# A six-layer decoder on one core: expert sums as seven block products, and two groups in turns

## The chip, the cores and the metric

The kernel runs on one core of a Trainium2 chip. Times are device microseconds (us) of one execution. Engines are named as the profile does: PE is TensorE (PEld its weight loads), DVE VectorE, ACT ScalarE, POOL GpSimd, SP the queue that issues most DMAs.

## What is computed

Sixteen sequences of 128 tokens with 256 features pass six sub-layers, each of the form `x = layernorm(x + f(x))`, all in float32:

- layer 0: attention with 16 heads of 64, causal mask, biases
- layer 1: 8 experts of hidden width 512; every token goes through every expert
- layer 2: two shared experts of hidden width 128 and 16 routed ones of 64 (top 2 by a softmax router)
- layer 3: attention with 16 heads of 16 and a band mask
- layer 4: cross attention with 16 heads of 16 to a context of 128 positions
- layer 5: 8 experts of hidden width 512 with GELU; again every token goes through every expert

The two layers that the change is about, cut to what matters:

```
# layer 1 (gate[b,s,e] sums the context's weights of the entries that chose e)
h   = relu(einsum('bsd,eid->bsei'))            # proj_in
out = einsum('eid,bsed->bsei', proj_out, h) summed over e with gate

# layer 5
h   = gelu(einsum('nd,edh->neh', xf, w1) + b1)
y   = einsum('neh,ehd->ned', h, w2) + b2
out = (y * norm_g[:, None, None]).sum(axis=1)
```

So each of these layers ends in a sum over 8 experts of a product of (tokens x 512) by (512 x 256).

## The kernel before

The sixteen sequences are four groups of four (`GB = 4`), a group has `T = 512` tokens. For a group, x is kept with tokens on partitions and, transposed, as xT with features on partitions. A layer of a group is a Python generator (`attention0`, `ensemble0`, `experts0`, `attention1`, `cross1`, `experts1`) that emits instructions and yields the TensorE time that the emitted piece should take. A `Weaver` mixes two such streams, main and side, in the proportion of the numbers given to it, and short streams (`tail`: the transposes of the next xT and the routing) go first when they are ready. `UNTIL` lets a stream wait until a given planned time. Layer n of a group starts when the tail of layer n - 1 has written xT (`written[g]`).

Main streams are the attentions: (0,0) alone first, then (0,1), (0,2), (0,3), then (3,g), (4,g) for each group. The side stream is called dense: (1,0), (2,0), (1,1), (2,1), (1,2), (2,2), (1,3), (2,3), then (5,0) to (5,3); what is left of it at the end runs alone. The pair is (layer, group). From the emitted program the framework then makes the queue of each engine, and two instructions of an engine needn't keep the order of the text, unless `keep_in_program_order` or `together` asks for it.

Layers 1 and 5 use `accumulate`. A piece i of 32 is one expert's quarter of hidden features. `hidden(i)` makes 128 hidden features of the 512 tokens (two matmuls of 512 columns at L289) and evicts them to SBUF (VectorE at L650 in layer 1, ScalarE at L813 in layer 5). Then four matmuls of 256 columns (L589) add this quarter's product to the four token blocks in two PSUM banks (tag M), over all 32 pieces. The result has tokens on partitions, and `Norm.add` reads it from PSUM at L265 or L267. Each matmul of the code is two records in the profile.

PSUM has 8 banks: H (2), M (2), O (2) and S (one buffer of two). Weights of an expert, up and down, lie in one slot of 8 KB a partition, of which there are three (`wp`, bufs=3); SP loads them in the order of the program as slots come free. Attention weights have three slots of their own.

`softmax` emits for a unit of scores: a minimum with the mask on VectorE (L311), a maximum (L317 or L319), one exponential a head on ScalarE (L325), a reciprocal on VectorE (L330), the product on GpSimd (L331). `weights_T` transposes e on TensorE (L51) and ScalarE copies it (L340). In layers 3 and 4 GpSimd also makes kb (L456), one head's keys spread over a block, ahead of the scores (L464).

Of the kernel before, what the change touches and what calls it, by code (L numbers as in the profile page):

```python
# [27 lines left out]
def kernel(ctx: ExitStack, tc: tile.TileContext, a: dict, out: bass.AP):  # L28
# [3 lines left out]
    wp = ctx.enter_context(tc.tile_pool(name="dense", bufs=3))  # L32
# [37 lines left out]
    def load_w(pool, name, *parts):  # L70
        w = pool.tile([P, 2048], F32, tag=pool.name, name=name)
        views, at = [], 0
        for part in parts:
            p_, r, c = part.shape
            v = w[:, at:at + r * c].rearrange("p (r c) -> p r c", r=r)
            nc.sync.dma_start(out=v, in_=part)
            views.append(v)
            at += r * c
        return views

    def load_quad(j):
# [3 lines left out]
            ap, f"wquad{j}", a["L0_attn_W_Q"][:, :, cols], a["L0_attn_W_K"][:, :, cols],  # L85
            a["L0_attn_W_V"][:, :, cols], a["L0_attn_W_O"][:, 2 * j:2 * j + 2, :],
        )

    def load_expert0(e):
        return load_w(wp, f"we0_{e}", a["L0_xattn_proj_in"][e], a["L0_xattn_proj_out"][e])  # L90

    def load_expert1(e):
        return load_w(wp, f"we1_{e}", a["L1_ffn_w1"][e], a["L1_ffn_w2"][e])

    def load_experts(t):

        if t == 0:
            return load_w(wp, "ws", a["L0_ffn_wg_s"], a["L0_ffn_wu_s"], a["L0_ffn_wd_s"])
        cols = slice((t - 1) * D, t * D)
        return load_w(  # L100
            wp, f"wr{t}", a["L0_ffn_wg_r"][:, :, cols], a["L0_ffn_wu_r"][:, :, cols],
            a["L0_ffn_wd_r"][:, 2 * t - 2:2 * t, :],
        )
# [61 lines left out]
    bv0 = spread("L0_attn_b_V")  # L165
    bo0 = spread("L0_attn_b_O")
    ctxs = cp.tile([P, NB, P], F32, tag="ctx", name="ctx")
    nc.gpsimd.dma_start(out=ctxs, in_=a["ctx_512"].rearrange("b k s -> k b s"))
# [4 lines left out]
    bv1 = spread("L1_xattn_bv")  # L173
# [17 lines left out]
    class Weaver:  # L191
# [23 lines left out]
        def weave(self, main, side=None, us=(1.0, 1.0)):  # L215
# [4 lines left out]
            while not main.over:  # L220
# [15 lines left out]
    def transposed(x, xT=None):  # L236
# [3 lines left out]
        for c in range(KC):  # L240
# [5 lines left out]
            else:  # L246
                nc.scalar.copy(xT[:, c, :], pt)
        return xT
# [42 lines left out]
    def values(xT, w, k, evict):  # L291

        v = p3.tile([P, GB, D], F32, tag="v", name="v")
        for b in range(0, GB, 2):
# [7 lines left out]
            evict(v[:, b:b + 2, :], pv)  # L302
# [3 lines left out]
    def softmax(s, seen):  # L306

        n = 2 * s.shape[2]
        if seen is not None:
            sm = p2.tile([P, n, P], F32, tag="s", name="sm")  # L310
            nc.vector.tensor_tensor(  # L311
                sm.rearrange("p (s h) k -> p s h k", s=2), s,
                seen.unsqueeze(1).unsqueeze(1).to_broadcast([P, 2, n // 2, P]), ALU.min,
            )
        nmax = sp.tile([P, n], F32, tag="nmax", name="nmax")
        if seen is not None:
            nc.vector.tensor_reduce(nmax, sm, AX.X, ALU.max, negate=True)  # L317
        else:
            nc.vector.tensor_reduce(  # L319
                nmax.rearrange("p (s h) -> p s h", s=2), s, AX.X, ALU.max, negate=True  # L320
            )
        e = p3.tile([P, n, P], F32, tag="p", name="e")
        total = sp.tile([P, n], F32, tag="total", name="total")
        for h in range(n):
            nc.scalar.activation(  # L325
                e[:, h, :], sm[:, h, :] if seen is not None else s[:, h // (n // 2), h % (n // 2), :],
# [16 lines left out]
    def attention0(x, xT, g):  # L343
# [4 lines left out]
        def project_quad(j):  # L348
# [16 lines left out]
            def with_bias(v, pv):  # L365
                nc.vector.tensor_tensor(
                    v, pv, bv0[:, j * D:(j + 1) * D].unsqueeze(1).to_broadcast([P, 2, D]),
                    ALU.add,
                )

            v = yield from values(xT, wv, KC, with_bias)
# [27 lines left out]
        for n in range(len(units) + 5):  # L399
# [17 lines left out]
            if m in eT:  # L417
# [14 lines left out]
                nc.scalar.copy(zT[m], pz)  # L432
# [14 lines left out]
    def attention16(x, qT, kT, v, wo, bo, seen):  # L447
# [22 lines left out]
        def weigh(b, c, eT):  # L470
# [15 lines left out]
            nc.scalar.activation(half_z, pz[:, 0, :], AF.Copy, scale=even[:, 0:1])  # L486
# [13 lines left out]
        for n in range(len(units) + 4):  # L500
            if n < 8:
                e[n] = yield from scores(*units[n])
                at["e", n] = weaver.now + 14.0
                yield 1.06
            m = n - 1
# [6 lines left out]
            m = n - 3  # L512
# [4 lines left out]
            m = n - 2  # L517
# [21 lines left out]
    def attention1(x, xT):  # L539
        wqkv, wo = load_w(ap, "wa1", a["L1_attn_Wqkv"], a["L1_attn_Wproj"])  # L540
# [7 lines left out]
        v = yield from values(xT, wqkv[:, :, 2 * D:3 * D], KC, nc.scalar.copy)  # L548
        yield from attention16(x, qT, kT, v, wo, bp1, band)

    def cross1(x, xT, g):
        wq, wk, wv, wo = load_w(
            ap, "wx1", a["L1_xattn_Wq"], a["L1_xattn_Wk"], a["L1_xattn_Wv"], a["L1_xattn_Wo"]
        )
        pc = bank("H")
        for b in range(GB):
            transpose(pc[:, b * P:(b + 1) * P], ctxs[:, g * GB + b, :])
        cT = p2.tile([P, 1, T], F32, tag="s", name="cT")
# [10 lines left out]
        def with_bias(v, pv):  # L569
            nc.vector.tensor_tensor(  # L570
                v, pv, bv1.unsqueeze(1).to_broadcast([P, 2, D]), ALU.add
            )

        v = yield from values(cT, wv, 1, with_bias)
        yield from attention16(x, qT, kT, v, wo, bo1, None)
# [22 lines left out]

    gates_of = {}

    def gates0(g):
# [5 lines left out]
        cx = ctxs[:, g * GB:(g + 1) * GB, :].rearrange("p b s -> p (b s)")  # L607
        held = dp.tile([8, T], F32, tag="gates", name="gatesd", bufs=NG)
        for q in range(2):
# [16 lines left out]
            sums = p3.tile([P, T], F32, tag="hT", name="sums")  # L626
# [8 lines left out]
    def ensemble0(x, xT, g):  # L635
        gates = {}
        w_exp0 = {}

        def hidden(i):
            e, c = divmod(i, 4)  # L640
            if c == 0:
                w_exp0[e] = load_expert0(e)
# [320 lines left out]
```

## Time and profile before

| what | us |
|---|---|
| median of 3 runs | 1867.82 |
| lowest, highest | 1865.88, 1871.24 |
| the profiled execution, its own time | 1863.81 |
| span of its records, first to last | 1862.1 |
| PE busy in it | 1805.6 |
| ACT busy | 750.1 |
| DVE busy | 648.7 |
| POOL busy | 363.0 |

The profile is one execution, recorded by the hardware profiler. A row of a group reads: line, engine, operation, tile written from tiles read, shape and count, then busy us and mean ns of one, then the idle time of the engine ahead of it and what ended that. A row of a table of stretches has busy us of PE, PEld, DVE, ACT and POOL with the number of instructions, the granted TensorE clock, the busy share of the DMA engines and GB/s. A row of waits names who waited for whom, with the total, the number of times and the longest.

### The profile page before, as it was taken

The page shows a single profiled execution, that of the slowest core. Times are in us where ns is not written, and L with a number is a line of the kernel's source. Part 1 is how long each engine was busy: PE and PEld are TensorE (multiplying, and loading weights), DVE is VectorE, ACT ScalarE, POOL GpSimd, SP SyncE. Part 2 cuts the span into 40 slices and gives each one's busy share as a digit, 9 for nine tenths or more (in the row PEclk, how much of TensorE's full clock was granted, in tenths as well). Part 3 has the DMA queues.
Part 4 walks back from the last instruction along what each step waited for, and adds up shares of the span by engine and source line. Part 5 has one row for each costly group of instructions (what it writes and reads, how often), then busy time and mean ns, then how long its engine had stood idle before and what let it go on. Part 6 is the DMA issues. An engine that isn't in the chain of part 4 may idle for free.

```text
span 1862.1 us, 21229 instructions
## 1 busy us (share of the span) xinstructions
PE 1805.6 (97%) x7794; PEld 1111.5 (60%) x7794; DVE 648.7 (35%) x1359; ACT 750.1 (40%) x2229; POOL 363.0 (19%) x297
## 2 busy tenths in 40 slices
PE   6999999999999999999899999899999999999998
PEld 3656666566666656656455665465565655556665
DVE  3453334434333525343425444333223222312101
ACT  2541222342312333241452423527748468475221
POOL 4210001121101112122332213223122122221000
PEclk9999999999999999999899999999999999999999
DMA  6021123122221132122123121121111111111220
GB/s 233 24 86 57 57 74 102 58 85 74 99 89 37 44 120 101 63 71 66 41 79 108 63 91 34 58 93 66 46 63 57 46 68 46 57 46 68 80 76 26
DMA packets 67272, 132.72 MB, mean 71 GB/s; under 512 B 6600, under 2 KB 34304, under 8 KB 67168
## 3 DMA queue, kind: packets, MB, share of 16 engines
q1 hardware_dynamic: 66240, 129.20, 20.5%
q0 software_dynamic: 928, 2.17, 0.4%
q8 instruction: 62, 1.02, 0.2%
q14 instruction: 42, 0.34, 0.1%
HBM read 129.04 MB, written 2.29 MB: 71 GB/s over the span
## 4 chain that ended last, share of the span: by engine, by line
PE 81%; issue 7%; ACT 5%; DVE 5%; DMA 1%; POOL 1%; SPq 0%; POOLq 0%; DVEq 0%; ACTq 0%
PE psH L289 34%; PE psM L589 23%; PE psH L298 4%; PE psO L51 4%; PE psS L464 3%; PE psH L393 3%; ACT e L325 2%; PE psS L384 2%; PE psO L426 2%; PE psO L476 2%; PE psH L495 1%; PE psH L51 1%; DMA wquad<-in_L_attn_W_Q 1%; ACT L325 1%; DVE x L281 1%
## 5 line engine op out<-in xcount | busy, mean ns | idle before, releaser
L589 PE MATMUL psM<-we,hT 128*128 128x256 f32 x2048 | 496.2, 383 | 3.1 <-ACT hT L813 3.1
L289 PE MATMUL psH<-xT,we 128*128 128x512 f32 x1024 | 488.3, 598 | 1.3 <-DVE hT L650 1.3
L589 PEld LDWEIGHTS psM<-we,hT 128*128 128x128 f32 x2048 | 380.7, 190 | 153.1 <-issue 95.1
L331 POOL TENSOR_TENSOR e<-e,inv 128x512 f32<-128x512 f32 (+1 forms) x128 | 188.2, 1471 | 792.6 <-DVE inv L330 728.2
L289 PEld LDWEIGHTS psH<-xT,we 128*128 128x128 f32 x1024 | 187.4, 190 | 159.9 <-issue 142.0
L325 ACT ACTIVATE e<-sm,nmax 128x128 f32<-128x128 f32 x512 | 198.5, 389 | 152.9 <-DVE nmax L317 152.5
L340 ACT COPY eT<-psO 128x512 f32<-128x512 f32 x192 | 106.0, 586 | 207.2 <-PE psO L51 206.7
L650 DVE SCALAR_TENSOR_TENSOR hT<-psH,gt 128x512 f32<-128x512 f32 x128 | 88.1, 689 | 214.1 <-PE psH L289 214.1
L813 ACT ACTIVATE hT<-psH,b 128x512 f32<-128x512 f32 x128 | 86.9, 687 | 177.1 <-PE psH L289 176.5
L289 PE MATMUL psH<-xT,wquad 128*128 128x512 f32 x256 | 117.7, 603 | 1.3 <-DVE qT L357 0.8
L51 PEld LDWEIGHTS psO<-ident,e 128*128 128x128 f32 x768 | 88.4, 143 | 49.4 <-issue 32.1
L51 PE MATMUL psO<-ident,e 128*128 128x128 f32 x768 | 111.0, 281 | 5.0 <-POOL e L331 4.9
L289 PE MATMUL psH<-xT,wr 128*128 128x512 f32 x256 | 115.8, 594 | 0.0
L456 POOL TENSOR_TENSOR kb<-kT,hm 128x512 f32<-128x512 f32 x64 | 66.9, 1046 | 189.4 <-PE psS L464 128.7
L330 DVE RECIPROCAL inv<-total 128x4 f32<-128x4 f32 (+1 forms) x128 | 23.9, 187 | 216.6 <-ACT e L325 214.0
L325 ACT ACTIVATE e<-psS,nmax 128x128 f32<-128x128 f32 x256 | 90.1, 379 | 21.3 <-DVE nmax L319 20.9
L325 ACT ACTIVATION_READ_ACCUMULATOR e<-sm,nmax 128x1 f32 x512 | 95.8, 187 | 0.0
L464 PE MATMUL psS<-kb,qT 64*128 64x512 f32 x256 | 84.5, 646 | 7.0 <-ACT e L325 6.7
L279 POOL TENSOR_TENSOR rstd<-ve,mhalf 128x4 f32<-128x4 f32 x24 | 24.3, 1012 | 310.0 <-DVE ve L277 309.4
L317 DVE TENSOR_REDUCE nmax<-sm 128x4 f32<-128x512 f32 (+1 forms) x96 | 82.8, 863 | 2.7
L289 PEld LDWEIGHTS psH<-xT,wquad 128*128 128x128 f32 x256 | 47.2, 191 | 58.3 <-issue 50.2
L289 PEld LDWEIGHTS psH<-xT,wr 128*128 128x128 f32 x256 | 48.0, 190 | 49.5 <-issue 46.3
(155 smaller groups left out, 1802.9 us busy)
## 6 DMA issues: line engine op xcount, KB each, us to landing
we<-in_L_ffn_w SPq DMA_DIRECT2D x64, 512.0 KB
we<-in_L_xattn_proj_in SPq DMA_DIRECT2D x32, 512.0 KB
we<-in_L_xattn_proj_out SPq DMA_DIRECT2D x32, 512.0 KB
gt<-gatesd SPq DMA_DIRECT2D x32, 256.0 KB
cw<-combd SPq DMA_DIRECT2D x64, 128.0 KB
wquad<-in_L_attn_W_Q SPq DMA_DIRECT2D x16, 256.0 KB
wquad<-in_L_attn_W_K SPq DMA_DIRECT2D x16, 256.0 KB
wquad<-in_L_attn_W_V SPq DMA_DIRECT2D x16, 256.0 KB
```

What stands on the lines that cost most here:

```text
L51: return nc.tensor.transpose(out_, in_, ident[:n, :n])
L289: mm(pt, lhsT=w[:, c, cols], rhs=xT[:, c, :], start=c == 0, stop=c == KC - 1)
L298: mm(pv[:, i, :], lhsT=xT[:, c, (b + i) * P:(b + i + 1) * P], rhs=w[:, c, :], start=c == 0, stop=c == k - 1,)
L317: nc.vector.tensor_reduce(nmax, sm, AX.X, ALU.max, negate=True)
L325: nc.scalar.activation(e[:, h, :], sm[:, h, :] if seen is not None else s[:, h // (n // 2), h % (n // 2), :], AF.Exp, bias=nmax[:, h:h + 1 ...
L331: nc.gpsimd.tensor_tensor(e, e, inv.unsqueeze(2).to_broadcast([P, n, P]), ALU.mult)
L340: return eT, nc.scalar.copy(eT, pt)
L456: nc.gpsimd.tensor_tensor(kb, kT[:, c, at].unsqueeze(1).to_broadcast([P, 4, P]), hm4.unsqueeze(2).to_broadcast([P, 4, P]), ALU.mult,)
L464: mm(s[:, k, :], lhsT=qT[rows, c, at], rhs=kb[rows].rearrange("p h k -> p (h k)"), start=True, stop=True,)
L589: step = mm(acc[b], lhsT=held[:, b * P:(b + 1) * P], rhs=down(i), start=i == 0 and b % 2 == 0, stop=i == n - 1, skip_group_check=True,)
L650: nc.vector.scalar_tensor_tensor(out=hT, in0=ph, scalar=0.0, in1=gates[e], op0=ALU.max, op1=ALU.mult)
L813: nc.scalar.activation(hT, ph, AF.Gelu, bias=b1[:, i:i + 1])
```

## The change

The sum of an expert's product is made by Strassen's scheme. Hidden features and output features are halved, and tokens too: a (tokens x hidden) by (hidden x features) product becomes two by two blocks, and seven products of blocks replace eight. One operand of a product is a sum or difference of two blocks of the hidden values, the other one of the down weights.

- The weight blocks (7 of 256 columns) are computed on GpSimd when the first group reaches an expert, stored to HBM from GpSimd's queue, and loaded from there by the other three groups (`load_blocks`).
- The hidden sums are made for an expert by VectorE, two of the five by GpSimd (`sums`).
- `multiply` issues the products in four phases, each of two products into one bank M (one in the last phase); VectorE then adds the bank to an accumulator in SBUF. The phases of expert e - 1 alternate with the four hidden pieces of expert e.
- At the end `products_end` combines the seven sums to four blocks, transposes them to tokens on partitions and adds them to x. It runs as a short stream, followed by the layer's tail.
- Up weights have three slots of 4 KB, blocks two slots of 7 KB. To make room, the context is loaded by group, the masked scores are written into e itself, and the biases of v go onto zT, which in layer 0 VectorE writes now instead of ScalarE.
- In layers 3 and 4 the transposes follow the scores two units later, not one.
- Dense order: two groups take layer 1 in turn, then both layer 2. The first main stream is (0,0), (0,1) with nothing beside it, and three mixed stretches of two groups follow.

The diff, cut to its core:

```diff
-    wp = ctx.enter_context(tc.tile_pool(name="dense", bufs=3))
+    wp = ctx.enter_context(tc.tile_pool(name="dense", bufs=2))
...
+    def load_up(name, *parts):
+        return load_w("up", 1024, name, *parts, bufs=3)
+
+    def load_down(name, *parts):
+        return load_w("down", 14 * P, name, *parts)
...
-    bv0 = spread("L0_attn_b_V")
+    bv0 = const("bv0", [P, 8], a["L0_attn_b_V"].rearrange("o (c p) -> p (o c)", p=P))
-    ctxs = cp.tile([P, NB, P], F32, tag="ctx", name="ctx")
-    nc.gpsimd.dma_start(out=ctxs, in_=a["ctx_512"].rearrange("b k s -> k b s"))
...
-            evict(v[:, b:b + 2, :], pv)
+            nc.vector.tensor_copy(v[:, b:b + 2, :], pv)
...
-                nc.scalar.copy(zT[m], pz)
+                nc.vector.tensor_tensor(
+                    zT[m], pz, bv0[:, 2 * j:2 * j + 2].unsqueeze(2).to_broadcast([P, 2, P]), ALU.add
+                )
...
-            m = n - 1
+            m = n - 2
             if m in e:
                 yield UNTIL, at["e", m]
...
+    def load_blocks(layer, e, g, w):
+        if (layer, e) in in_hbm:
+            got, = load_down("wb", in_hbm[layer, e])
+            return got.rearrange("p s (q d) -> p s q d", q=2)
+        raw, = load_up("raw", w)
+        raw = raw.rearrange("p (q l) (j d) -> p q l j d", l=2, j=2)
+        t = wp.tile([P, 7, 2 * P], F32, tag="down", name="wb0")
+        blocks = t.rearrange("p s (q d) -> p s q d", q=2)
+        for s, (_, (one, two, op)) in enumerate(PRODUCTS):
+            if two is None:
+                step = nc.gpsimd.tensor_copy(blocks[:, s], raw[:, :, one[0], one[1], :])
+            else:
+                step = nc.gpsimd.tensor_tensor(
+                    blocks[:, s], raw[:, :, one[0], one[1], :], raw[:, :, two[0], two[1], :], op
+                )
+            if s == 0:
+                together(step, *transposed_by[g])
+        held = dp.tile([P, 7, 2 * P], F32, tag=f"wb{layer}", name="wbd", bufs=8)
+        nc.gpsimd.dma_start(out=held, in_=t)
...
+        def sums(e, phase):
+            t = None
+            for s in range(2 * phase, min(2 * phase + 2, 7)):
+                one, two, op = PRODUCTS[s][0]
+                if two is None:
+                    parts[e, s] = half(e, one)
+                    continue
+                if t is None:
+                    t = p3.tile([P, 2, 2, 2 * P], F32, tag="cm", name="cm")
+                parts[e, s] = t[:, s % 2]
+                engine = nc.gpsimd if s in (3, 5) else nc.vector
+                engine.tensor_tensor(t[:, s % 2], half(e, one), half(e, two), op)
+
+        def multiply(e, phase):
+            pm = bank("M").rearrange("p (s t) -> p s t", s=2)
+            slots = range(2 * phase, min(2 * phase + 2, 7))
+            for q in range(2):
+                for s in slots:
+                    step = mm(
+                        pm[:, s % 2, :], lhsT=blocks[e][:, s, q, :], rhs=parts[e, s][:, q, :],
+                        start=q == 0 and s % 2 == 0, stop=q == 1, skip_group_check=True,
+                    )
...
+            to = acc[:, slots[0]:slots[-1] + 1, :]
+            if e == 0:
+                nc.vector.tensor_copy(to, pm[:, :len(slots), :])
+            else:
+                nc.vector.tensor_tensor(to, pm[:, :len(slots), :], to, ALU.add)
+
+        for e in range(9):
+            if e < 8:
+                blocks[e] = blocks_of(e)
+                h[e] = p2.tile([P, 4, T], F32, tag="h", name="h")
+            if e > 0:
+                sums(e - 1, 0)
+                sums(e - 1, 1)
+            for c in range(4):
+                if e < 8:
+                    hidden(h[e][:, c, :], up[e], e, c)
+                    yield 1.72
+                    if c == 1 and e < 7:
+                        up[e + 1] = load_up_of(e + 1)
+                if e > 0:
+                    if c < 2:
+                        sums(e - 1, c + 2)
+                    multiply(e - 1, c)
+                    yield 1.72 if c < 3 else 0.86
+        finish(acc)
+
+    def products_end(acc, norm, scale):
+        t = p3.tile([P, 2, 2, 2 * P], F32, tag="cm", name="y")
...
+        nc.gpsimd.tensor_tensor(c12, m3, m5, ALU.add)
+        nc.vector.tensor_tensor(c11, m4, m5, ALU.subtract)
+        nc.vector.tensor_tensor(c11, c11, m1, ALU.add)
+        nc.vector.tensor_tensor(c11, c11, m7, ALU.add)
+        nc.gpsimd.tensor_tensor(c21, m2, m4, ALU.add)
+        nc.vector.tensor_tensor(c22, m1, m2, ALU.subtract)
+        nc.vector.tensor_tensor(c22, c22, m3, ALU.add)
+        nc.vector.tensor_tensor(c22, c22, m6, ALU.add)
...
-        (1, 0), (2, 0), (1, 1), (2, 1), (1, 2), (2, 2), (1, 3), (2, 3),
+        (1, 0), (1, 1), (2, 0), (2, 1), (1, 2), (1, 3), (2, 2), (2, 3),
         (5, 0), (5, 1), (5, 2), (5, 3),
     ))
-    weaver.weave(Stream(chain((0, 0))))
+    weaver.weave(Stream(chain((0, 0), (0, 1))))
     weaver.short.append(Stream(sum_biases()))
...
+    weaver.weave(Stream(chain((0, 2), (0, 3))), dense, (81.0, 150.0))
+    weaver.weave(Stream(chain((3, 0), (4, 0), (3, 1), (4, 1))), dense, (68.0, 150.0))
+    weaver.weave(Stream(chain((3, 2), (4, 2), (3, 3), (4, 3))), dense, (68.0, 150.0))
+    weaver.weave(dense, last=True)
```

## The prediction

> **What bounds the kernel now.** I read the page's head and its chain first, then the time order of TensorE in the stretch with the least company, then tables by stretch, last the waits of the engines that get new work.
>
> ```profile
> span 1862.1 us, 21229 instructions
> ...
> PE 1805.6 (97%) x7794; PEld 1111.5 (60%) x7794; DVE 648.7 (35%) x1359; ACT 750.1 (40%) x2229; POOL 363.0 (19%) x297
> ...
> PE 81%; issue 7%; ACT 5%; DVE 5%; DMA 1%; POOL 1%; SPq 0%; POOLq 0%; DVEq 0%; ACTq 0%
> ```
>
> TensorE is busy for 97% and makes up 81% of the chain; no other engine passes 40%. Busy is not yet peak, so the price of a matmul comes from starts, in the stretch in which layer 5 runs alone:
>
> ```profile
> 1759.68 1.89 PE L589 MATMUL psM<-we,hT 128*128 128x256 f32 x8
> 1761.41 1.88 PE L289 MATMUL psH<-xT,we 128*128 128x512 f32 x4
> 1763.13 1.89 PE L589 MATMUL psM<-we,hT 128*128 128x256 f32 x8
> ```
>
> Each matmul of the code is two records. Eight records, four matmuls of 256 columns, take 1.73 us from start to start: 0.431 us each; two of 512 columns take 1.72 us. Here TensorE does not wait at all. Where it does wait shows in a table of stretches (busy columns PE, PEld, DVE, ACT, POOL, then the granted clock):
>
> ```profile
> 895.00:920.00 25.00, 17.29 (x92) 9.40 (x91) 14.28 (x41) 15.12 (x61) 9.71 (x7) 0.80 0.11 29
> 1150.00:1180.00 30.00, 23.03 (x111) 12.77 (x109) 20.12 (x57) 15.71 (x62) 11.79 (x8) 0.89 0.09 28
> 1750.00:1850.00 100.00, 100.00 (x350) 66.26 (x349) 0.00 (x0) 20.08 (x30) 0.00 (x0) 1.00 0.15 54
> ```
>
> The first two are changes of layer: an expert sum of a group has ended, its routing isn't there yet, and only attention is left to run. TensorE idles 7.7 and 7.0 us, at a lower clock. VectorE does nothing in the third.
>
> **The change part by part.**
>
> *Seven products for eight.* An expert pass of layer 1 or 5 (8 experts, 4 groups, 2 layers: 64 passes) issues 14 down matmuls of 256 columns for 16. Shape and operands' sizes stay, so the price stays: 64 x 2 x 0.431 = -55.2 us, on the path since TensorE bounds. A pass falls from 8 x 1.72 = 13.8 to 12.9 us.
>
> *Transposes at the end.* The sums now come out with features on partitions: 8 transposes for each of 8 group-layers. Four transposes of e start 0.43 us ahead of what follows (168.37 to 168.80 in the time order), so 64 x 0.11 = +7.0 us.
>
> *Evictions and sums.* Before, PSUM held the sum over all experts. Now each pass evicts four phases into SBUF (three of 512 columns, one of 256) and makes five sums of hidden halves, three on VectorE, two on GpSimd. The nearest rows:
>
> ```profile
> L311 DVE TENSOR_TENSOR sm<-psS,causal 128x512 f32<-128x512 f32 x64 | 44.1, 689 | 51.4 <-PE psS L384 51.4
> L265 DVE TENSOR_TENSOR x<-psH,x 128x256 f32<-128x256 f32 x96 | 40.3, 420 | 83.4 <-PE psH L495 48.6 <-PE psH L393 34.2
> L756 POOL TENSOR_TENSOR hT<-sg,cw x32: 1262/1270/1383, 361.1 to 1247.8; 128x512 f32<-128x512 f32 x32
> ```
>
> VectorE: 3 x 0.69 + 0.42 + 3 x 0.69 = 4.6 us a pass, 292 us in all; with 64 zT evictions taken from ACT (64 x 0.42 = 27), v (6) and the final combination (8 x 6 x 0.42 = 20) it goes from 649 to about 994 us, 55% of the span. GpSimd: 128 sums x 1.27 = 163 us; and for the first group of a layer 7 block operations of 256 elements (about 0.65 us each, half of the 512 row) and a store issue (the 1 MB ctx load cost 1.19 us) for 16 experts, 89 us: 363 to some 625 us, 34%. What hides this is the time of a pass: each sum is made one phase ahead and has about 5.2 us of TensorE work (three pieces of 1.72) before it is read, each bank two phases. If that cover is gone, 1 us of lateness a pass costs 64 us.
>
> *Whether they come late* is the unknown term. Two waits block the queues concerned:
>
> ```profile
> POOL e L331 <- DVE inv L330: 728.2, 117, 29.5
> DVE inv L330 <- ACT e L325: 214.0, 82, 8.1
> ```
>
> GpSimd stands at the softmax product, 6.2 us on average, VectorE at the reciprocal. A sum queued behind either waits with it, and the products that read it wait on TensorE with all that follows. Against it: the queue need not follow the text of the program. In one stretch VectorE ran
>
> ```profile
> 1062.51 1.22 DVE L317 TENSOR_REDUCE nmax<-sm 128x8 f32<-128x1024 f32 x1
> 1063.65 0.68 DVE L650 SCALAR_TENSOR_TENSOR hT<-psH,gt 128x512 f32<-128x512 f32 x1
> ...
> 1067.21 0.19 DVE L330 RECIPROCAL inv<-total 128x8 f32<-128x8 f32 x1
> ```
>
> two expert evictions between a reduction and its reciprocal (one lies in the gap shown by dots), though the code has these in one call. So most sums can be queued ahead of a blocked product. Bounds: 0, or if each of the 68 sums of the 34 passes beside layers 3 and 4 comes 1.1 us late, +75 us. I take +12, nearer to the low end, because VectorE at 35% with the same blocking leaves TensorE only scattered gaps today.
>
> A rule speaks against the change here. The trace first: the GpSimd product with two SBUF inputs has 1262 to 1383 ns, so nothing blocked it; but in this kernel hardly any VectorE instruction has two large SBUF inputs. The Trainium skill, SBUF — State Buffer, section "Who interferes with whom", says that a VectorE instruction with two SBUF inputs and a GpSimd instruction that reads SBUF exclude each other for a whole instruction. The three VectorE sums are of that kind. By the rule two GpSimd sums a pass hold VectorE up by at most 2 x 1.27 = 2.5 us; if TensorE felt all of it, 64 x 2.5 = +163 us. By the row and the 5.2 us of cover it is 0. I take 0 beyond the 12 us above.
>
> *Loads.* For each pass before: 512 KB up and 512 KB down into one of three slots. After: up into one of three, down as blocks into one of two. SP issues 64 up, 16 raw and 48 block loads (896 KB) against 128 before, and the 32 gate loads one expert earlier; ctx comes in 8 loads of 256 KB on SP instead of one on GpSimd's queue. GpSimd issues 16 stores of 896 KB; each waits for seven block operations, and these for the raw load, so a softmax product queued behind them waits too (in the 12). Traffic grows from 133 MB to about 166 MB, some 91 GB/s where the first 50 us moved 217. A block load needs about 4.2 us at that rate, and its slot comes free a whole pass (12.9 us) before use: 0. If SP comes late to it because an attention load blocks the queue, the excess over 8 us is TensorE's; bound 0 to +20, value 0.
>
> *Turns of two groups.* Dense order becomes (1,0), (1,1), (2,0), (2,1): while a group's sum is combined, normalized and routed, the other group's experts run. That takes away the two stretches above: -15 us (bounds -5, if another wait is next, to -20 with their slow clock). What is late next: attention's own pipeline, where transposes wait for e. There a unit more of distance removes some of the scattered waits: -3 (0 to -10). Against it, group 1's attention 0 now runs without experts beside it, and so a second pipeline runs empty uncovered: +3 (0 to +8; the stretch 100 to 150, with the first such end, has 2.4 us of idle PE). Leaving less for the dense end costs nothing, as both mixtures are bounded by TensorE.
>
> *Start and end.* The 1 MB ctx load and the 512 KB bias spread leave the start, where TensorE waits 6.2 and 3.2 us for x: -2 (0 to -5). At the end the last phase is evicted (0.42), six VectorE operations combine (6 x 0.42) and 8 transposes follow (0.9) before the old tail: +4.5. Shorter last passes without hidden pieces between phases: +1. ACT loses 28 us of copies, worth 0, as it is not late there.
>
> Sum: -55.2 + 7.0 + 12 - 15 - 3 + 3 - 2 + 4.5 + 1 = -47.7 us against the profiled execution's 1863.8 us (span 1862.1): 1816. That execution was 4.0 us below the median of the runs, 1867.8, so I forecast **1820 us**.
>
> **The rivals.**
>
> *Work is saved, lateness eats most of it.* VectorE at 55%, more beside attention, delays softmax as much as sums: 20 to 42 us more than I put. For: it had 35%. Against: cover of 5.2 us. 1840 to 1862.
>
> *More is gained.* Waits of under 1 us scattered over attention go too, by the deeper pipeline and the ACT copies that left: 1785 to 1800. Against: most of these are switches between shapes, which stay.
>
> *GpSimd's queue becomes the bound.* Place: passes beside layers 3 and 4, sums behind a softmax product of 1.9 us that waits 5 us for its reciprocal. Price 75 us or more for the 12: 1820 + 63 = 1883, slower. It decides from (47.7 + 12) / 68 = 0.9 us of lateness a sum on. For: the 728 us of blocked GpSimd. Against: order need not be the text's, and the 5.2 us.
>
> That fewer matmuls are not issued can be ruled out: 14 for 16 stands in the code.
>
> **How the numbers follow.** My case 0.61, more gained 0.10, eaten 0.20, GpSimd 0.09. A measurement can tell about 0.3%, 5.6 us: faster means under 1862. Of the eaten case a fifth ends within that bound: faster 0.87, same 0.04, slower 0.09. The range from 1788 to 1862 leaves out about 0.05 below and 0.13 above.
>
> **What would show it.** Right: 1792 records of down matmuls from we for 2048, at the same spacing where layer 5 runs alone; no stretch with 7 us of idle PE at a change of layer; VectorE near 990 us, GpSimd near 620. Wrong: PE waiting for cm sums made on GpSimd, M banks waiting for VectorE, or block loads that land late.

## The result, and the profile after

| kernel | median, us | ratio to the kernel before | 95% interval |
|---|---|---|---|
| before, same chip | 1869.53 | 1 | |
| changed | 1838.13 | 0.9834 | 0.9816 to 0.9853 |

The change is 1.7% faster: 31 us where I forecast 48. The page of the changed kernel, its span, busy times and chain:

```profile
span 1836.1 us, 21774 instructions
...
PE 1757.7 (96%) x7602; PEld 1068.6 (58%) x7602; DVE 1050.7 (57%) x1927; ACT 731.0 (40%) x2161; POOL 673.8 (37%) x568
...
PE 74%; DVE 11%; ACT 8%; issue 3%; POOL 2%; DMA 2%; SPq 0%; POOLq 0%; DVEq 0%; ACTq 0%
```

TensorE has 48 us less of busy time, but the span of the profiled execution fell by 26, so TensorE is idle for 22 us more. VectorE went from 5% to 11% of the chain: some time that TensorE gave up is now spent waiting for VectorE. In the stretch where layer 5 runs alone nothing of that is to be seen. The first hidden piece of one expert, and that of the next, in order of time:

```profile
1751.34 1.88 PE L288 MATMUL psH<-xT,we 128*128 128x512 f32 x4
...
1764.25 1.88 PE L288 MATMUL psH<-xT,we 128*128 128x512 f32 x4
```

A pass takes 12.91 us, as forecast (12.9), though VectorE and GpSimd are at work now. The table of stretches, with the two of before and two more:

```profile
895.00:920.00 25.00, 20.15 (x98) 12.46 (x97) 19.95 (x42) 9.21 (x40) 11.03 (x9) 0.93 0.21 69
1150.00:1180.00 30.00, 29.95 (x148) 16.69 (x145) 10.49 (x18) 27.13 (x74) 15.93 (x11) 1.00 0.20 64
1390.00:1420.00 30.00, 23.80 (x90) 12.53 (x89) 19.47 (x36) 17.53 (x55) 13.37 (x11) 0.83 0.20 67
1750.00:1800.00 50.00, 50.00 (x173) 32.52 (x172) 23.41 (x27) 10.99 (x16) 13.80 (x8) 1.00 0.30 106
```

The stretch at 1150 is full, the one at 895 has 4.9 us of idle PE instead of 7.7, and there is a new one: 6.2 us idle between 1390 and 1420, at a clock of 0.83. Two waits make it up:

```profile
1394.38 1.65 PE L51 MATMUL psH<-ident,y 128*128 128x128 f32 x8 [2.54 <-DVE y L712]
...
1413.16 2.08 PE L465 MATMUL psS<-kb,qT 64*128 64x512 f32 x4 [3.63 <-issue]
```

The first is the combination of the first group's sum of layer 5 (y). For the second, ahead of scores of attention, the profile names no releaser. The table of waits names what TensorE waits for elsewhere (total us, times, longest):

```profile
POOL e L335 <- DVE inv L334: 376.4, 104, 10.3
...
PEld psO L477 <- ACT eT L344: 25.9, 35, 1.8
...
PEld psH L288 <- DVE h L774: 8.4, 9, 1.9
PEld psH L51 <- DVE y L712: 8.1, 3, 3.4
...
PE psH L51 <- DVE y L712: 6.1, 3, 2.5
...
PEld psM L671 <- DVE acc L681: 4.3, 10, 1.6
...
PEld psM L671 <- POOL cm L663: 1.2, 2, 0.9
...
PE psM L671 <- POOL cm L663: 0.5, 1, 0.5
```

The largest of TensorE's that an engine ended, for ScalarE's copies eT, is not new; before it was

```profile
PEld psO L476 <- ACT eT L340: 24.7, 51, 0.9
```

A row of PEld is a weight load that waits, which matmuls before it can still cover; a row of PE is idle time of TensorE. Added up over all rows of PE, the idle time that VectorE ended went from 13.7 us before to 35.0, that of ScalarE from 13.0 to 14.0, that of GpSimd from 4.9 to 1.4. So the new idle time of 22 us is TensorE waiting for VectorE, in many short waits: for evicted hidden values (h), for the combination (y), for a free bank (acc), for the queries and the x of the next layer, and hardly at all for the hidden sums (cm), whoever makes them. The blocked softmax product on GpSimd went from 728 to 376 us. And the sums themselves are longer than the nearest rows said (minimum, median, maximum in ns):

```profile
L663 DVE TENSOR_TENSOR cm<-h x192: 659/1126/2379, 225.5 to 1818.3; 128x512 f32<-128x512 f32 x192
L663 POOL TENSOR_TENSOR cm<-h x128: 1262/1714/1873, 225.5 to 1817.8; 128x512 f32<-128x512 f32 x128
```

Both minima are near the forecast's durations, 0.69 and 1.27 us. The medians are 0.44 us above these. The time order shows when:

```profile
1751.45 0.69 DVE L663 TENSOR_TENSOR cm<-h 128x512 f32<-128x512 f32 x1 [1.80 <-ACT h L933]
1751.49 3.45 POOL L663 TENSOR_TENSOR cm<-h 128x512 f32<-128x512 f32 x2 [9.52 <-PE psH L288]
1752.06 0.42 DVE L681 TENSOR_TENSOR acc<-psM,acc 128x256 f32<-128x256 f32 x1
1752.39 3.10 DVE L663 TENSOR_TENSOR cm<-h 128x512 f32<-128x512 f32 x2
```

Two sums of each engine side by side take 1.72 us each on GpSimd and 1.55 on VectorE.

### The profile page after: what moved, and what is told of

Read it like the earlier page. It is cut to its first block, busy times and chain, and to the rows that moved or that the text cites. A ratio compares the mean times of both kernels' runs of the same rounds, so it can differ in the third digit from the quotient of the medians.

```text
span 1836.1 us, 21774 instructions
## 1 busy us (share of the span) xinstructions
PE 1757.7 (96%) x7602; PEld 1068.6 (58%) x7602; DVE 1050.7 (57%) x1927; ACT 731.0 (40%) x2161; POOL 673.8 (37%) x568
## 3 DMA queue, kind: packets, MB, share of 16 engines
q1 hardware_dynamic: 70464, 150.17, 25.5%
## 4 chain that ended last, share of the span: by engine, by line
PE 74%; DVE 11%; ACT 8%; issue 3%; POOL 2%; DMA 2%; SPq 0%; POOLq 0%; DVEq 0%; ACTq 0%
PE psH L288 33%; PE psM L671 16%; ACT e L329 4%; PE psH L305 4%; PE psM L592 4%; PE psO L51 4%; PE psH L391 3%; DVE cm L663 3%; PE psS L382 2%; PE psS L465 2%; PE psO L424 2%; PE psO L477 2%; DVE nmax L324 1%; PE psH L51 1%; ACT L933 1%
## 5 line engine op out<-in xcount | busy, mean ns | idle before, releaser
L663 POOL TENSOR_TENSOR cm<-h 128x512 f32<-128x512 f32 x128 | 205.3, 1621 | 356.1 <-DVE h L774 164.6
L671 PE MATMUL psM<-cm,wb 128*128 128x256 f32 x1280 | 313.9, 385 | 2.1 <-DVE acc L681 1.6
L329 ACT ACTIVATE e<-e,nmax 128x128 f32<-128x128 f32 x512 | 198.6, 389 | 258.6 <-DVE nmax L324 258.2
L671 PEld LDWEIGHTS psM<-cm,wb 128*128 128x128 f32 x1280 | 238.5, 190 | 99.3 <-issue 65.4
L663 DVE TENSOR_TENSOR cm<-h 128x512 f32<-128x512 f32 x192 | 219.2, 1165 | 40.3 <-ACT h L933 37.9
L681 DVE TENSOR_TENSOR acc<-psM,acc 128x512 f32<-128x512 f32 x224 | 138.5, 619 | 174.8 <-PE psM L671 174.2
L671 PE MATMUL psM<-h,wb 128*128 128x256 f32 x512 | 124.3, 385 | 0.0
L671 PEld LDWEIGHTS psM<-h,wb 128*128 128x128 f32 x512 | 96.5, 192 | 32.8 <-issue 18.7
L288 PE MATMUL psH<-xT,wg 128*128 128x512 f32 x256 | 115.5, 594 | 0.0
L329 ACT ACTIVATION_READ_ACCUMULATOR e<-e,nmax 128x1 f32 x512 | 95.7, 187 | 0.0
```

The source lines that it names most:

```text
L288: mm(pt, lhsT=w[:, c, cols], rhs=xT[:, c, :], start=c == 0, stop=c == KC - 1)
L329: nc.scalar.activation(e[:, h, :], s[:, h // (n // 2), h % (n // 2), :], AF.Exp, bias=nmax[:, h:h + 1], accum_out=total[:, h:h + 1],)
L663: engine.tensor_tensor(t[:, s % 2], half(e, one), half(e, two), op)
L671: step = mm(pm[:, s % 2, :], lhsT=blocks[e][:, s, q, :], rhs=parts[e, s][:, q, :], start=q == 0 and s % 2 == 0, stop=q == 1, skip_group_ch ...
L681: nc.vector.tensor_tensor(to, pm[:, :len(slots), :], to, ALU.add)
```

## The experiments

All ratios are to the kernel before on the same chip; "worth" is the difference of ratios times 1866 us, so that kernels timed beside different executions of before compare. The changed kernel stands at 0.9834, or 31 us under before. An interval of about 0.0015 on each side is 3 us.

**The new order alone.** The kernel before, with the dense order and the main stretches of the change:

```diff
-        (1, 0), (2, 0), (1, 1), (2, 1), (1, 2), (2, 2), (1, 3), (2, 3),
+        (1, 0), (1, 1), (2, 0), (2, 1), (1, 2), (1, 3), (2, 2), (2, 3),
...
-    weaver.weave(Stream(chain((0, 0))))
+    weaver.weave(Stream(chain((0, 0), (0, 1))))
...
+    weaver.weave(Stream(chain((0, 2), (0, 3))), dense, (81.0, 158.0))
+    weaver.weave(Stream(chain((3, 0), (4, 0), (3, 1), (4, 1))), dense, (68.0, 158.0))
+    weaver.weave(Stream(chain((3, 2), (4, 2), (3, 3), (4, 3))), dense, (68.0, 158.0))
```

> The kernel before with the new order alone: dense order and three mixed stretches of two groups as in the change, (0,0) and (0,1) with nothing beside them (shares 158 for 150, as a pass still has eight products). No block products. Theory A (the prediction's step): turns take away the two stretches of 7 us of idle TensorE and cost 3 us for a second uncovered attention, so about 12 us faster than before, near 1857. Theory B: a group of attention that runs alone leaves gaps of about 20% against 8% beside experts, which costs 15 to 20 us and eats what the turns gain: 1865 to 1880, same as before or slower.

Measured: 1851.7 us, ratio 0.9921 (0.9907 to 0.9935), 15 us faster than before. Theory A holds. Its two stretches:

```profile
895.00:920.00 25.00, 25.00 (x127) 15.82 (x126) 13.79 (x44) 10.38 (x42) 6.85 (x5) 1.00 0.17 64
1150.00:1180.00 30.00, 29.01 (x128) 15.34 (x127) 13.38 (x35) 22.18 (x68) 13.37 (x10) 1.00 0.23 70
```

Of 14.7 us of idle PE, 1.0 is left, and the granted clock is full. The 15 us agree with this step of the sum, -12 for turns with their second uncovered attention. The gaps did not only vanish, though: over the whole span idle PE fell by 3.7 us alone (56.5 to 52.8), and the rest of what the span lost is shorter busy time, at a mean clock of 0.996 for 0.994. Part of the idle time moved into the second attention that runs without experts. From 105 to 215 us, before, with the new order alone, and in the changed kernel:

```profile
105.00:215.00 110.00, 107.89 (x471) 66.50 (x470) 43.37 (x80) 24.76 (x86) 9.64 (x9) 1.00 0.20 65
...
105.00:215.00 110.00, 104.82 (x613) 65.38 (x612) 57.49 (x119) 52.01 (x190) 19.77 (x19) 1.00 0.18 56
...
105.00:215.00 110.00, 101.71 (x566) 61.96 (x564) 64.33 (x136) 42.54 (x155) 26.49 (x28) 0.98 0.27 84
```

That is 3.1 us more of idle PE, which is the forecast's +3, but 6.2 more in the changed kernel.

**The products in the old order.** The changed kernel with the old dense order and seven stretches of one group:

```diff
-        (1, 0), (1, 1), (2, 0), (2, 1), (1, 2), (1, 3), (2, 2), (2, 3),
+        (1, 0), (2, 0), (1, 1), (2, 1), (1, 2), (2, 2), (1, 3), (2, 3),
...
-    weaver.weave(Stream(chain((0, 0), (0, 1))))
+    weaver.weave(Stream(chain((0, 0))))
...
+    weaver.weave(Stream(chain((0, 1))), dense, (81.0, 103.0))
+    weaver.weave(Stream(chain((0, 2))), dense, (81.0, 99.0))
+    weaver.weave(Stream(chain((0, 3))), dense, (81.0, 99.0))
+    weaver.weave(Stream(chain((3, 0), (4, 0))), dense, (68.0, 103.0))
+    weaver.weave(Stream(chain((3, 1), (4, 1))), dense, (68.0, 99.0))
+    weaver.weave(Stream(chain((3, 2), (4, 2))), dense, (68.0, 99.0))
+    weaver.weave(Stream(chain((3, 3), (4, 3))), dense, (68.0, 103.0))
```

> The changed kernel with the dense order and the main stretches of the kernel before (one group a stretch, shares scaled to the shorter passes: 103 and 99). Products, slots and the deeper pipeline of layers 3 and 4 stay. Theory A: the turns were worth 12 us, so 1850. Theory B: the turns were worth nothing or less, so 1838 or below, down to 1825.

Measured: 1865.98 us, ratio 0.9998 (0.9988 to 1.0009). Both theories missed. With the order of before, seven products for eight gain nothing, so the order is worth 31 us to the products and 15 us without them. The page:

```profile
span 1864.3 us, 21802 instructions
...
PE 1774.9 (95%) x7602; PEld 1073.5 (58%) x7602; DVE 1062.2 (57%) x1927; ACT 701.7 (38%) x2137; POOL 674.6 (36%) x568
```

Its table of stretches, at the two changes from layer 1 to layer 2 (from:to and length, then busy us of PE, PEld, DVE, ACT and POOL, the granted clock, the DMA share and GB/s):

```profile
885.00:932.00 47.00, 36.36 (x188) 20.62 (x187) 31.45 (x76) 24.55 (x101) 16.36 (x12) 0.89 0.10 31
1165.00:1212.00 47.00, 36.41 (x160) 22.84 (x158) 39.16 (x89) 17.66 (x76) 21.22 (x18) 0.89 0.14 45
```

TensorE is busy for 31 us less than before in a longer span; at each of these two changes 10.6 us of PE are idle (47.00 - 36.36, 47.00 - 36.41), where before had 7.7 and 7.0 in its stretches. So with the products the gap at a change of layer is wider, and the turns, which put another group's work there, have more to cover. The two gaps are some 6 us of the 31. Over the whole span, TensorE is idle for 11.0 us more than in the changed kernel and busy for 17.2 us more with the same 7602 records, at a mean clock of 0.987 for 0.993 (table at the end of this section).

**Group 1's attention beside experts.**

```diff
-    weaver.weave(Stream(chain((0, 0), (0, 1))))
+    weaver.weave(Stream(chain((0, 0))))
...
-    weaver.weave(Stream(chain((0, 2), (0, 3))), dense, (81.0, 150.0))
+    weaver.weave(Stream(chain((0, 1), (0, 2), (0, 3))), dense, (81.0, 104.0))
```

> The changed kernel, but (0,0) alone first and then (0,1), (0,2), (0,3) beside layer 1 and 2 (shares 81 to 104, so that as much dense work lies in these as now). Theory B (gaps of the second attention alone): 15 to 20 us faster than the changed kernel, near 1820, with the gaps between 105 and 216 us gone. Theory A (the second attention costs 3 us; the loss lies in late sums and evictions beside attention): within 5 us of 1838.

Measured: 1853.34 us, ratio 0.9932 (0.9918 to 0.9945), 18 us slower than the changed kernel. Theory B falls, and A didn't expect a loss either. That the first two groups have no expert beside them does not lose here. Which stretch the 18 us come from is not settled by this run; of the 15.2 us by which its profiled span is longer, 3.4 are idle PE and 11.8 longer busy time, at a mean clock of 0.988.

**All hidden sums on VectorE.**

```diff
-                engine = nc.gpsimd if s in (3, 5) else nc.vector
+                engine = nc.vector
```

> The changed kernel with all five hidden sums on VectorE, none on GpSimd. If VectorE's sums of 1.13 us median and GpSimd's of 1.71 (nearest rows said 0.69 and 1.27) are long because each keeps the other from SBUF, the sums of VectorE fall to 0.69 us and VectorE's busy time stays near 1050 us (192 x 0.45 us less, 128 x 0.69 more). If that loss was on the path, 5 to 15 us faster than 1838; if the cover of 5 us a phase hid it, within 4 us. Rival: two SBUF inputs of 512 cost VectorE 1.13 us by themselves: the mean stays above 1.1 and the time rises by 5 us or more, as VectorE gets 5 x 1.13 a pass.

Measured: 1827.6 us, ratio 0.9798 (0.9780 to 0.9816), 7 us faster than the changed kernel by ratios, 2.0% faster than before. It is the fastest of the kernels that compute everything. The sums, and the busy times:

```profile
L663 DVE TENSOR_TENSOR cm<-h x320: 639/684/2411, 223.3 to 1810.9; 128x512 f32<-128x512 f32 x160
```

```profile
PE 1757.7 (96%) x7602; PEld 1071.7 (59%) x7602; DVE 1061.1 (58%) x2055; ACT 739.3 (40%) x2167; POOL 478.2 (26%) x440
```

The median fell to 0.68 us. VectorE makes 320 sums for 192 in 10 us more of busy time: GpSimd's 196 us of help had saved VectorE nothing worth having. The rival, that two SBUF inputs are slow by themselves, falls. Of TensorE's idle time VectorE now ends 25.5 us instead of 35.0.

**What each part of the new VectorE and GpSimd work costs.** Four kernels, each the changed one with something left out.

No block making (the first group's blocks are the raw weights, loaded by SP):

```diff
-        raw, = load_up("raw", w)
-        raw = raw.rearrange("p (q l) (j d) -> p q l j d", l=2, j=2)
         t = wp.tile([P, 7, 2 * P], F32, tag="down", name="wb0")
+        nc.sync.dma_start(out=t[:, 0:4], in_=w)
+        nc.sync.dma_start(out=t[:, 4:7], in_=w[:, 0:3])
         blocks = t.rearrange("p s (q d) -> p s q d", q=2)
-        for s, (_, (one, two, op)) in enumerate(PRODUCTS):
...
-                together(step, *transposed_by[g])
```

> The changed kernel without the seven block operations on GpSimd: the first group's raw weights go by SP straight into the block slot (1.75 times the bytes), the store to HBM stays. This leaves out the weight blocks' sums. Theory V (VectorE, at 57%, comes late with whatever TensorE waits for; GpSimd hardly matters): within 5 us of 1838. Theory G (GpSimd's queue, blocked by raw loads and 80 us of block operations for the first group): 10 to 20 us faster, most of it beside layers 3 and 4 between 1225 and 1400 us.

Measured: 1833.74 us, ratio 0.9831 (0.9816 to 0.9846): no difference from 0.9834. GpSimd's block making costs nothing that can be told, unless the larger loads that replace it cost as much, and theory G loses its first part.

No hidden sums:

```diff
-                if two is None:
-                    parts[e, s] = half(e, one)
-                    continue
+                parts[e, s] = half(e, one)
+                continue
```

> The changed kernel without the five hidden sums: every product reads a block of h itself. This leaves out the sums of the hidden operand. TensorE's work is the same. VectorE loses 219 us, GpSimd 205. Theory V: 12 to 20 us faster (1818 to 1826), of which 10 are the collision that sums on VectorE alone already took away. Theory G: the same size, but with VectorE's evictions left as they are no gain beyond 10 us, so 1828.

Measured: 1813.92 us, ratio 0.9730 (0.9714 to 0.9746), 19 us faster than the changed kernel; the sums on VectorE alone had won 7 of them.

No accumulation over experts:

```diff
-            else:
-                nc.vector.tensor_tensor(to, pm[:, :len(slots), :], to, ALU.add)
```

> The changed kernel in which only the first expert's phases are copied from PSUM; those of the other seven are multiplied and then dropped. This leaves out the sum over experts. VectorE loses 138 us of 1051; the waits of TensorE for a free bank M go too. Theory V: 8 to 15 us faster (1823 to 1830), by shorter waits for h, e, x and zT, not by those for acc (2.4 us in all). Theory G: within 4 us of 1838.

Measured: 1825.91 us, ratio 0.9794 (0.9779 to 0.9808), 7 us faster than the changed kernel by the ratios and 12 by the medians. Each ratio has some 3 us of interval on either side, so that their difference is known to 4 or 5: theory V's lower end (8) and G's 4 both lie within it, and this run alone doesn't part them.

Neither sums nor accumulation (the two diffs above together):

> Both the five hidden sums and the accumulation over experts left out, so neither operand sums nor the sum over experts are made; TensorE issues the same 14 matmuls a pass. If lateness of VectorE is all that kept the change from its 48 us on top of the 14 of the new order, the time goes to about 1866 - 14 - 48 = 1804; the single omissions gave -24 and -12, so 1802 by addition. Rival: other new parts (block making, two slots for blocks, the combination at the end) hold 10 us or more: 1812 or above.

Measured: 1804.71 us, ratio 0.9668 (0.9654 to 0.9683), 62 us faster than before. That agrees with the forecast's 48 us of TensorE work on top of 15 us of order. Its page has VectorE at 40% and TensorE again at 97%:

```profile
span 1802.6 us, 21083 instructions
...
PE 1751.8 (97%) x7602; PEld 1068.4 (59%) x7602; DVE 713.3 (40%) x1511; ACT 730.8 (41%) x2161; POOL 454.4 (25%) x440
```

TensorE is busy for 46.4 us less than with the order alone (1798.2), so nearly all of the 48 us is there. Against the changed kernel its idle time fell from 78.4 to 50.8 us, the part that VectorE ended from 35.0 to 17.6. This is the measure of lateness: without the new VectorE work most of the waits go.

**An eighth product.**

```diff
-                for s in slots:
+                for s in (*slots, *((7,) if phase == 3 else ())):
...
-                        pm[:, s % 2, :], lhsT=blocks[e][:, s, q, :], rhs=parts[e, s][:, q, :],
+                        pm[:, s % 2, :], lhsT=blocks[e][:, min(s, 6), q, :], rhs=parts[e, min(s, 6)][:, q, :],
...
-                    yield 1.72 if c < 3 else 0.86
+                    yield 1.72
```

> The changed kernel with an eighth product in the last phase that nobody reads (it repeats the seventh's operands into the free half of the bank): two more matmuls of 256 columns in each of 64 passes, as the kernel before had, no more work for any other engine. If TensorE's work is the path throughout, 64 x 2 x 0.431 = 55 us slower, 1893. If late VectorE work were the path in a good part of the span, the extra matmuls would fill gaps that exist anyway: 20 to 40 us slower.

Measured: 1899.92 us, ratio 1.0178 (1.0161 to 1.0195), 64 us slower than the changed kernel (interval some 5 us). TensorE's work is on the path throughout, at 0.50 us a matmul. Why that is above the 0.431 of the steady stretch is open; the run also plans a longer last phase, which shifts the mixture a little.

**The shallow pipeline.** Layers 3 and 4 as before, transposes one unit behind the scores:

```diff
-                at["e", n] = weaver.now + 16.0
+                at["e", n] = weaver.now + 14.0
...
-            m = n - 2
+            m = n - 1
             if m in e:
...
```

> The changed kernel with the pipeline of layers 3 and 4 as before (transposes one unit behind the scores, 14 us instead of 16). The prediction put the deeper one at -3 us, so 1841. If VectorE's lateness makes e late beside experts, the deeper pipeline holds more: 1848 or above. If it holds nothing, 1838.

Measured: 1874.74 us, ratio 1.0043 (1.0031 to 1.0055), 39 us slower than the changed kernel and slower than before. A stretch of its table near the end:

```profile
1700.00:1750.00 50.00, 42.66 (x202) 26.69 (x201) 27.31 (x70) 24.28 (x76) 16.26 (x12) 0.86 0.17 58
```

Here 7.3 us of PE are idle, at a clock of 0.86: attention ends late, and the last group's experts can't start before it. After that gap the same instructions take longer. Eight records of 512 columns of layer 5 before it and after it, then the stretches that they lie in, at clocks of 1.00 and 0.73:

```profile
1696.94 3.60 PE L288 MATMUL psH<-xT,we 128*128 128x512 f32 x8
...
1746.91 5.08 PE L288 MATMUL psH<-xT,we 128*128 128x512 f32 x8
```

```profile
1696.00:1701.00 5.00, 5.00 (x17) 2.46 (x14) 2.56 (x6) 4.97 (x20) 1.48 (x2) 1.00 0.12 49
1746.00:1753.00 7.00, 6.75 (x15) 3.38 (x16) 4.05 (x17) 2.78 (x4) 1.01 (x1) 0.73 0.00 0
```

The profiled execution, the fastest of this kernel, has a span 30.0 us above the changed kernel's: 9.0 of it are idle PE and 21.0 longer busy time. Without the deeper pipeline, which I had put at -3, the change is 8 us slower than before.

**Two attempts at more.** From the kernel with all sums on VectorE. The first lets layers 3 and 4 take turns as well:

```diff
-    weaver.weave(Stream(chain((3, 0), (4, 0), (3, 1), (4, 1))), dense, (68.0, 150.0))
-    weaver.weave(Stream(chain((3, 2), (4, 2), (3, 3), (4, 3))), dense, (68.0, 150.0))
+    weaver.weave(Stream(chain((3, 0), (3, 1), (4, 0), (4, 1))), dense, (68.0, 150.0))
+    weaver.weave(Stream(chain((3, 2), (3, 3), (4, 2), (4, 3))), dense, (68.0, 150.0))
```

> All hidden sums on VectorE, and layers 3 and 4 in turns of two groups as well: (3,0), (3,1), (4,0), (4,1). If changes of layer in the attention stream still leave TensorE waiting (gaps at 732, 909 and 1596 us in the changed kernel, each with a transpose of x or a context behind it), 4 to 10 us faster than 1827.6; if experts fill these anyway, within 4 us.

Measured: 1855.22 us, ratio 0.9950 (0.9935 to 0.9965), 28 us slower than without it. A miss. Of 25.9 us of span, 7.8 are more idle PE and 18.1 longer busy time, at a mean clock of 0.987 for 0.993; what sets it off is open.

The second moves work to ScalarE:

```diff
-                nc.vector.tensor_tensor(
-                    zT[m], pz, bv0[:, 2 * j:2 * j + 2].unsqueeze(2).to_broadcast([P, 2, P]), ALU.add
-                )
+                for i in range(2):
+                    nc.scalar.activation(
+                        zT[m][:, i, :], pz[:, i, :], AF.Identity, bias=bv0[:, 2 * j + i:2 * j + i + 1]
+                    )
...
-            v = yield from values(xT, wv, KC)
+            v = yield from values(xT, wv, KC, nc.scalar.copy)
...
-                nc.vector.tensor_copy(to, pm[:, :len(slots), :])
+                nc.scalar.copy(to, pm[:, :len(slots), :])
```

> All hidden sums on VectorE, and from VectorE to ScalarE: zT of layer 0 (two activations of 0.38 us for one VectorE instruction of 0.42), v of layer 0, and the first expert's copies out of PSUM; together 27 + 22 + 20 us. If VectorE's load is the cause, 4 to 8 us faster than the 1827.6 of sums on VectorE alone, as leaving out 138 us gave 12. If not, or if ScalarE now comes late to the next matmul, 1827 or above.

Measured: 1835.24 us, ratio 0.9834 (0.9819 to 0.9848), 7 us slower than the sums on VectorE alone, although VectorE's busy time fell from 1061 to 998 us. Who waited for zT, in this kernel and then in that one:

```profile
  PEld psO L424: 8.8, 27
...
  PEld psH L391: 7.6, 15
  PE psH L391: 3.9, 9
```

```profile
  PEld psH L391: 2.9, 5
...
  PE psH L391: 1.3, 3
```

TensorE now waits for zT on ScalarE, where two activations of 0.36 us, in a queue with the exponentials, take the place of one VectorE instruction of 0.42. The idle time of TensorE that VectorE ended stayed as it was (25.5 and 25.6 us), and what ScalarE ended grew from 16.1 to 19.4. That is about half of the 7 us, which are known to 5; as three things moved at once, the rest is open. So busy time of VectorE is no measure of the loss by itself: 63 us less of it won nothing.

**Where TensorE's time went.** One profiled execution of each, in us. Idle is span less busy time; the next column adds up the rows of PE in the waits that VectorE ended; the clock is the mean granted one, as a share of full speed.

| kernel | span | PE busy | PE idle | ended by VectorE | clock |
|---|---|---|---|---|---|
| before | 1862.1 | 1805.6 | 56.5 | 13.7 | 0.994 |
| new order alone | 1851.0 | 1798.2 | 52.8 | 10.3 | 0.996 |
| changed | 1836.1 | 1757.7 | 78.4 | 35.0 | 0.993 |
| products in the old order | 1864.3 | 1774.9 | 89.4 | 50.4 | 0.987 |
| group 1 beside experts | 1851.3 | 1769.5 | 81.8 | 36.8 | 0.988 |
| shallow pipeline | 1866.1 | 1778.7 | 87.4 | 42.9 | 0.989 |
| sums on VectorE | 1826.1 | 1757.7 | 68.4 | 25.5 | 0.993 |
| the same, layers 3 and 4 in turns | 1852.0 | 1775.8 | 76.2 | 36.5 | 0.987 |
| neither sums nor accumulation | 1802.6 | 1751.8 | 50.8 | 17.6 | 0.995 |

The four kernels at 0.987 to 0.989 lose twice: 3 to 11 us more of idle PE than the kernel they were made from, and 12 to 21 us more of busy time for the same 7602 records. By an estimate from these rows, a mean clock lower by 0.004 to 0.006 over some 1850 us is 7 to 11 us of that busy time; the rest is not located. In stretches of 50 us of these nine traces, every one at a clock below 1 also had idle PE (0.8 us or more), but not the other way round: the first 50 us of before have 16.4 us of idle PE at a clock of 1.00. No run here tests what makes the clock fall.

## Why the prediction was right, and where it was off

The forecast was 1820 us, 48 below before; the measured 1838 is 31 below, inside the range of 1788 to 1862. Of the signs that I had named, the down matmuls have 1280 + 512 = 1792 records, the spacing where layer 5 runs alone held, and no stretch shown at a change of layer has 7 us of idle PE. Two came out higher: VectorE is busy for 1051 us and not near 990, GpSimd for 674 and not near 620. The hidden sums are the largest part of this: they took 219 us on VectorE and 205 on GpSimd, where 192 x 0.69 and 128 x 1.27 give 132 and 163. (The parts that I wrote out for GpSimd, 363 + 163 + 89, add up to 615 and not 625.)

- **Seven products for eight, -55.2, and transposes, +7.0:** shown as a sum. A pass has 12.91 us, the eighth product costs 64 us, and without VectorE's new work TensorE is busy for 46 us less than with the order alone. The transposes were not tested by themselves.
- **Lateness, +12:** the term that was mis-sized. Leaving out sums and accumulation wins 31 us, which is what it costs. 19 of it belong to the sums, 7 to the accumulation, and together they cost 4 more, which is within what these ratios can tell. The bounds of 0 and 75 held it, but my reason for the low end ("VectorE at 35% with the same blocking leaves TensorE only scattered gaps today") said nothing of VectorE at 57%. The place was another one too. I had TensorE wait for hidden sums that stand behind a blocked softmax product, and it waits 0.5 us for them; late are VectorE's other results, which now share its queue with 219 us of sums and 158 us of evictions into acc.
- **The rule on two SBUF inputs, weighed against the row:** I followed the row and put 0 for it. The rule (Trainium skill, SBUF — State Buffer, "Who interferes with whom") was right that the two kinds of sum hold each other up: 1.13 us for 0.69 on VectorE, 1.71 for 1.27 on GpSimd. It was worth 7 us on the path, known to 5, not 163, since where layer 5 runs alone the cover held. My row, a GpSimd product beside VectorE instructions with one SBUF input, was not the case in question.
- **Turns, -15 and +3:** the order alone agrees, 15 us faster where these terms said 12. But the step took the two parts for independent: the products without the order gain nothing.
- **The deeper pipeline, -3:** wrong in size. It holds 39 us in the changed kernel. I read its worth from the waits of the kernel before, and not from one with 400 us more work in VectorE's queue. That this is why it grew is argued: no run has the deeper pipeline without the products.
- **GpSimd's queue as the bound:** falls. TensorE is idle for 1.4 us in all for results of GpSimd, and its block making costs nothing that can be told.
- **Start, end and loads:** not tested one by one. They balance in the sum: -15 (order) - 48 (work) + 31 (lateness) = -32, for the 31 measured. The sum leaves the deeper pipeline out, and taken one at a time the order is worth 15 or 31 us and the pipeline 39, so it is one way to book the time and not the only one.

That the total came out in the range was in part luck. Without the new order the change gains nothing, without the deeper pipeline it loses 8 us; the sum had these at -12 and -3, and no term for what they do together with the products.

The time lies near the case "eaten", just outside its lower edge of 1840. Its mechanism, new VectorE work that makes other results late, is what the runs show, 19 us above the 12 that I put. It took half of the 62 us that work and order had to give, and not nearly all; and softmax, which the rival named, was not late at its end: TensorE's idle time before the transposes of e fell from 4.9 to 0.9 us.

## What to carry to other kernels

Work taken from the bounding engine and put on others returns only as far as every result that it waits for stays early: measure that by leaving the new work out, not by the busy share of the engine that took it over. A helper engine may be none: here two fifths of the sums on GpSimd made the others slower by nearly as much as it took, and one engine alone was faster. A change of order or of pipeline depth that seems worth little before a change can be what carries it after. And where gaps came up here, the same instructions also took longer, at a lower granted clock, so compare busy time as well as idle time.

## What the runs showed of the hardware

That VectorE and GpSimd hold each other up when both sum from SBUF was stated by the rule; the size was not expected. From 1751.45 to 1755.49, which is 4.04 us, the lines above have three sums on VectorE and two on GpSimd, and one accumulation from PSUM (L681, 0.42 us) besides. One after another, by their undisturbed durations, the sums alone would take 3 x 0.69 + 2 x 1.27 = 4.61 us. So two engines together made hardly more than one at a time would: most of the time that one works, the other waits, which shows as 1.72 us for 1.27 and 1.55 for 0.69. It is not all of the time, as it would be if one excluded the other for whole instructions: 4.04 is less than 4.61.

The hidden sums aren't the only ones. In the combination ahead of TensorE's wait of 2.54 us, a VectorE operation with two SBUF inputs, which takes 0.42 us as a median, took 1.78 beside GpSimd's softmax product:

```profile
1390.83 2.02 POOL L335 TENSOR_TENSOR e<-e,inv 128x1024 f32<-128x1024 f32 x1
...
1391.35 1.78 DVE L714 TENSOR_TENSOR y<-acc 128x256 f32<-128x256 f32 x1
```

Moving the hidden sums to VectorE does not remove this: there the longest of these operations still takes 2.12 us.
